# Recommendation model with target attention: the order of a pipelined kernel left to the tile scheduler, with the label's head and the top network no longer spread over steps

## The chip, the cores and the metric

The kernel runs on one core of a Trainium2 chip. The metric is device time in microseconds of one execution. A core has five engines that each work through their own queue of instructions in order and wait for each other on semaphores: TensorE (PE, matmuls; its weight loads are shown apart as PEld), VectorE (DVE), ScalarE (ACT), GpSimd (POOL, which here issues the indirect gathers) and SyncE (SP, which issues plain DMAs). TensorE reads SBUF and writes PSUM; VectorE and ScalarE read PSUM.

## The reference

For each of 16384 samples there are 69 item numbers and one label. Cut to what matters:

```python
u  = emb[batch_user]                      # (16384, 69, 96)
ql = emb[batch_label[:, 0]]               # (16384, 96)
z  = concat([q, u, q - u, q * u], -1)     # q is ql, repeated for the 69 items
h  = dice(z @ W1 + b1, a1)                # 64 wide
att = (h @ W2 + b2) @ W3 + b3             # one number for each item
pre = where(batch_user < ITEM_NUM, u * att, 0)
pooled = einsum('gf,bfe->bge', window, pre)   # ten groups of items, sums
x = concat([pooled, ql], -1)              # 11 * 96 wide
h = dice(bn(x @ Wf1 + bf1), af1)          # 200 wide
h = dice(bn(h @ Wf2 + bf2), af2)          # 80 wide
return h @ Wf3 + bf3
```

`dice(x, a)` is `x * (a + (1 - a) * sigmoid(x))` up to a tiny constant. All data is float32.

## The kernel before

The samples are taken in 128 blocks of 128; eight blocks make a round, whose item and label numbers are loaded with one DMA (`load_ids`, L416; `round_of`). A block has 69 tiles of 128 items. The tiles go in 18 chunks of four (the last two have three and two), and two chunks make a pair: nine pairs a block, 1152 in all. In names such as "pair 3" the pair's place in its block is meant, from 0 to 8.

Since `z @ W1` is linear in `u` for a fixed label, each sample has its own matrix: `A + Wp * q`, 96 x 64, with a row for the part that depends on the label alone. These matrices are `M`, one tile of 97 x 128 x 64 for a block, in two buffers. VectorE fills it in five pieces with two instructions each (`build`, L257 and L263), cut by the table `BUILD`. Ahead of that comes the label's head: the gather of the label's rows (`head_gather`), their transpose and its copy to `qT` (`head_turn`, L237 and L239), and the row `c` (`head_row`, L245 and L247), which goes through DRAM to the last row of `M` (L249 and L251, both issued by SP).

A pair goes through these steps:

- `fetch`: eight gathers by POOL into `u` (L222, ten buffers), each of 128 rows; eight transposes by TensorE into `ptr` (L274, PSUM, two buffers); two copies by ScalarE to one of four `uT` (L276).
- `hidden`: one product for each sample that the pair touches, with the sample's matrix as weights, into `ph` (L288); the two chunks use the two column halves of TensorE in turn. ScalarE makes `g` in two steps (L304, L305), VectorE makes `y` (L306).
- `attend`: TensorE makes `patt` (L316), VectorE makes `w` and `rw` (L326, L334).
- `pool`: TensorE multiplies `u` with `rw` into `acc` (L358), which gathers the group sums; VectorE copies a full `acc` to `pooled` (L366). With this the buffer of `u` is free for the gathers ten pairs on.

After a block's last pair the top network follows: `top1` (L377 on TensorE, L385 to L389), `top2` (L397 to L401), `top3` (L406, L408). All of `patt`, the head's products and those of the top network share two PSUM buffers of one tag, `m`.

The loop at the end of the kernel writes the order of the work by hand. It stands in `with tc.manual_schedule():`, in which each engine's queue has its instructions in the order of the program text. Step `i` does `pool` of pair i-3, `attend` of pair i-2, `hidden` of pair i-1, then, where a block ended, one of the top network's three parts (at distances 4, 5 and 6), then `fetch` of pair i. The next block's head goes at the end of the steps with pair 2, 3 and 4, its builds at the end of those with pairs 4 to 8. So in TensorE's queue each step has eight `acc`, four `patt`, some 17 `ph` and eight transposes (the first three in two passes each).

Of the kernel before, what the change touches and what calls it, by code (L numbers as in the profile page):

```python
# [30 lines left out]
F32 = mybir.dt.float32  # L31
# [24 lines left out]
NPR = NCH // 2  # L56
NCOL = NB * (NT + 1)

BUILD = {4: (0, 26), 5: (26, 52), 6: (52, 78), 7: (78, 103), 8: (103, 128)}

GROUPS = [(0, 43), (43, 86), (86, 128)]

# [23 lines left out]
def rec_kernel(  # L86
# [23 lines left out]
    nc = tc.nc  # L110
# [101 lines left out]
    bpool = ctx.enter_context(tc.tile_pool(name="bpool", bufs=2))  # L212
# [6 lines left out]
    ps_m = ctx.enter_context(tc.tile_pool(name="ps_m", bufs=2, space=PSUM))  # L219

    def gather(dst, index):
        nc.gpsimd.indirect_dma_start(  # L222
            out=dst,
            out_offset=None,
            in_=emb,
            in_offset=bass.IndirectOffsetOnAxis(ap=index, axis=0),
        )

    def head_gather(n, ids):

        q = bpool.tile([P, E], F32, tag="q", name=f"q{n}")
        gather(q, ids[:, NB * NT + n % NB : NB * NT + n % NB + 1])
        return q

    def head_turn(n, q):
        pq = ps_m.tile([E, BLK], F32, tag="m", name=f"pq{n}")
        nc.tensor.transpose(pq, q, ident)  # L237
        qT = qpool.tile([E, BLK], F32, tag="qT", name=f"qT{n}")
        nc.vector.tensor_copy(qT, pq)  # L239
        return qT  # L240

    def head_row(n, qT):

        pc = ps_m.tile([BLK, H1], F32, tag="m", name=f"pc{n}")
        nc.tensor.matmul(pc, qT, Cq, start=True, stop=True)  # L245
        c = bpool.tile([BLK, H1], F32, tag="c", name=f"c{n}")
        nc.vector.tensor_add(c, pc, b1b)  # L247
        cd = dpool.tile([BLK, H1], F32, tag="cd", name=f"cd{n}")
        nc.sync.dma_start(out=cd, in_=c)  # L249
        M = bpool.tile([E + 1, BLK, H1], F32, tag="M", name=f"M{n}")  # L250
        nc.sync.dma_start(out=M[E : E + 1], in_=cd.rearrange("(o n) h -> o n h", o=1))  # L251
        return M

    def build(qT, M, a, b):

        m = M[0:E, a:b, :]
        nc.vector.tensor_tensor(  # L257
            m,
            Wp.to_broadcast([E, b - a, H1]),
            qT[:, a:b].rearrange("e (m o) -> e m o", o=1).to_broadcast([E, b - a, H1]),  # L260
            ALU.mult,
        )
        nc.vector.tensor_tensor(m, m, A.to_broadcast([E, b - a, H1]), ALU.add)  # L263

    def fetch(i, bi, pr, ids):

        u = upool.tile([P, 8, E], F32, tag="u", name=f"u{i}")
        uT = uTs[i % len(uTs)]
        for j in range(2):
            ch = CHUNKS[2 * pr + j]  # L270
            ptr = ps_tr.tile([E, 512], F32, tag="tr", name=f"ptr{i}_{j}")
            for k, t in enumerate(ch):
                gather(u[:, 4 * j + k, :], ids[:, bi * NT + t : bi * NT + t + 1])
                nc.tensor.transpose(ptr[:, k * P : (k + 1) * P], u[:, 4 * j + k, :], ident)  # L274
            n = len(ch) * P
            nc.scalar.copy(uT[0:E, j * 512 : j * 512 + n], ptr[:, 0:n])  # L276
        return u
# [90 lines left out]
                            acc[gi][:, 0 : (b - a) * G].rearrange("e (s g) -> e s g", g=G),  # L368
                        )

    def top1(n, pooled, qT):
        x1 = bpool.tile([DH, 2, BLK], F32, tag="x1", name=f"x1_{n}")
        g1 = bpool.tile([DH, 2, BLK], F32, tag="g1", name=f"g1_{n}")
        p1 = ps_m.tile([DH, 2, BLK], F32, tag="m", name=f"p1_{n}")
# [15 lines left out]
        return x1  # L390

    def top2(n, x1):
        x2 = bpool.tile([D2, BLK], F32, tag="x2", name=f"x2_{n}")
        g2 = bpool.tile([D2, BLK], F32, tag="g2", name=f"g2_{n}")
        p2 = ps_m.tile([D2, BLK], F32, tag="m", name=f"p2_{n}")
# [6 lines left out]
        return x2  # L402

    def top3(n, x2, res):
        p3 = ps_m.tile([1, BLK], F32, tag="m", name=f"p3_{n}")
        nc.tensor.matmul(p3, wf3, x2, start=True, stop=True)  # L406
        bi = n % NB
        nc.vector.tensor_scalar(res[:, bi * BLK : (bi + 1) * BLK], p3, bf3c, None, ALU.add)  # L408
        if bi == NB - 1:
            nc.sync.dma_start(out=out_v[n // NB : n // NB + 1], in_=res)  # L410

    out_v = out.rearrange("(n b) o -> n (o b)", n=NIT)

# [2 lines left out]
        nc.sync.dma_start(out=ids, in_=idx[it : it + 1].rearrange("o p n -> (o p) n"))  # L416
        return ids

    rounds = {}

    def round_of(n):

        it = n // NB
        if it not in rounds:
            ids = load_ids(it)
            mask = ipool.tile([P, NB * NT], F32, tag="mask", name=f"mask{it}")
            nc.vector.tensor_scalar(mask, ids[:, 0 : NB * NT], float(ITEM_NUM), None, ALU.is_lt)
            rounds[it] = ids, mask, ipool.tile([1, NB * BLK], F32, tag="res", name=f"res{it}")
        return rounds[it]

    total = NBLK * NPR
    qs, qTs, Ms, us, ys, rws, accs, x1s, x2s = ({} for _ in range(9))

    def part(i, back):

        return divmod(i - back, NPR) if 0 <= i - back < total else None

    with tc.manual_schedule():
        qs[0] = head_gather(0, round_of(0)[0])
        qTs[0] = head_turn(0, qs.pop(0))  # L440
        Ms[0] = head_row(0, qTs[0])
        for a, b in BUILD.values():
            build(qTs[0], Ms[0], a, b)
        for i in range(total + 6):
            if at := part(i, 3):
                n, pr = at
                if pr == 0:
                    accs[n] = {"pooled": bpool.tile([E, G, BLK], F32, tag="pooled", name=f"pooled{n}")}
                pool(i - 3, pr, us.pop(i - 3), rws.pop(i - 3), accs[n])
            if at := part(i, 2):  # L450
                n, pr = at
                rws[i - 2] = attend(i - 2, n % NB, pr, round_of(n)[1], ys.pop(i - 2))
            if at := part(i, 1):
                n, pr = at
                ys[i - 1] = hidden(i - 1, pr, Ms[n])
            if (at := part(i, 4)) and at[1] == NPR - 1:
                n = at[0]
                x1s[n] = top1(n, accs.pop(n)["pooled"], qTs.pop(n))
            if (at := part(i, 5)) and at[1] == NPR - 1:
                x2s[at[0]] = top2(at[0], x1s.pop(at[0]))  # L460
            if (at := part(i, 6)) and at[1] == NPR - 1:
                top3(at[0], x2s.pop(at[0]), round_of(at[0])[2])
            if at := part(i, 0):
                n, pr = at
                us[i] = fetch(i, n % NB, pr, round_of(n)[0])
                if n + 1 < NBLK:
                    if pr == 1:
                        round_of(n + 1)
                    if pr == 2:
                        qs[n + 1] = head_gather(n + 1, round_of(n + 1)[0])  # L470
                    if pr == 3:
                        qTs[n + 1] = head_turn(n + 1, qs.pop(n + 1))
                    if pr == 4:
                        Ms[n + 1] = head_row(n + 1, qTs[n + 1])
                    if pr in BUILD:
                        build(qTs[n + 1], Ms[n + 1], *BUILD[pr])


# [39 lines left out]
```

## Time and profile before

Three runs took 14158.46, 14157.09 and 14178.55 us (median 14158.46).

| | before |
|---|---|
| profiled execution's own time | 14158.46 us |
| its span, first to last instruction | 14156.7 us |
| instructions | 187662 |
| mean granted TensorE clock | 0.575 |
| TensorE matmuls, busy | 10058.7 us, 71% |
| POOL busy | 9627.4 us, 68% |
| VectorE busy | 4441.9 us, 31% |
| ScalarE busy | 3142.9 us, 22% |
| gathers of `u` | 8832, mean 1073 ns |
| gathers of `q` | 128, mean 1145 ns |
| DMA, mean | 33 GB/s |

In a group of the profile there stand the line, engine and operation, what is written and read, and the count; then busy time in us and the mean of one in ns; then the idle time of that engine just before such instructions, with what ended most of it. "issue" is time in which an engine waited for nothing that the profile shows, and "remote" stands where the releaser was not found. In a list of waits there stand the waiting engine and line, the releaser, total us, times, and the longest. In a timeline there stand start and length in us, then the idle time before and its releaser. In a table of windows there stand, for each stretch of the span, its length and each engine's busy time with the number of instructions.

### The profile page before, as it was taken

To read this page: it belongs to the slowest core of one execution; us is meant where nothing else is said; L and a number is where in the kernel's file an instruction comes from. 1 tells how busy PE (TensorE), PEld (TensorE's weight loads), DVE (VectorE), ACT (ScalarE), POOL (GpSimd) and SP (SyncE) were. 2 spreads that over 40 slices of the span, in tenths; PEclk is the share of its full clock that TensorE was granted. 3 is DMA by queue.
4 is the path that set the end of the run, shared out by engine and by line. 5 is a ranking of instruction groups with operands and counts; after the bars stand their busy time and mean duration, and the time that the engine had idled before them with its cause. 6 is when DMAs were issued, how large, how long until landed. Compare 5 with 4: busy or idle time off the path is not lost.

```text
span 14156.7 us, 187662 instructions
## 1 busy us (share of the span) xinstructions
PE 10058.7 (71%) x80260; PEld 9342.3 (66%) x80260; DVE 4441.9 (31%) x6564; ACT 3142.9 (22%) x5506; POOL 9627.4 (68%) x8966
## 2 busy tenths in 40 slices
PE   5776677766777677767776677767677677777777
PEld 4676666666676666666676666666666666666666
DVE  2332333323333233323333333323332333323332
ACT  1222222222222222222222222222222222222222
POOL 6667666666676666766667666666666666676665
PEclk8555555555555555555555555555555555555555
DMA  1111111111111111111111111111111111111111
GB/s 37 33 33 33 33 33 33 34 33 33 33 33 34 33 34 33 33 34 33 33 33 34 33 33 33 33 33 33 33 33 33 33 33 33 33 34 33 33 32 25
DMA packets 311848, 467.53 MB, mean 33 GB/s; under 512 B 164156, under 2 KB 165340, under 8 KB 310892
## 3 DMA queue, kind: packets, MB, share of 16 engines
q0 software_dynamic: 286720, 440.98, 14.9%
q1 hardware_dynamic: 22634, 13.19, 0.4%
q8 instruction: 636, 10.42, 0.3%
q10 hardware_dynamic: 1666, 1.37, 0.0%
q14 instruction: 192, 1.57, 0.0%
HBM read 450.69 MB, written 4.26 MB: 32 GB/s over the span
## 4 chain that ended last, share of the span: by engine, by line
PE 41%; another core or an unknown queue 20%; POOL 17%; issue 12%; DVE 5%; ACT 3%; DMA 2%; SPq 0%; POOLq 0%; ACTq 0%; DVEq 0%
POOL u L222 17%; PE acc L358 10%; PE ph L288 9%; PE patt L316 8%; PE ptr L274 7%; PE p L377 4%; DMA u<-in_emb,ids 1%; DVE M L263 1%; DVE M L257 1%; DVE y L306 1%; ACT g L305 1%; ACT uT L276 1%; PE p L397 1%; ACT g L304 1%
## 5 line engine op out<-in xcount | busy, mean ns | idle before, releaser
L222 POOL DMA_INDIRECT u<-in_emb,ids x8832 | 9480.2, 1073 | 4261.9 <-issue 2428.5
L316 PE MATMUL patt<-v,y 128*128 128x2 f32 x8704 | 1814.7, 327 | 2543.8 <-DVE y L306 1985.8
L316 PEld LDWEIGHTS patt<-v,y 128*128 128x128 f32 x8704 | 1758.8, 297 | 2594.3 <-DVE y L306 2035.9
L288 PE MATMUL ph<-uT,M 97*64 97x69 f32 (+7 forms) x37120 | 2540.4, 304 | 897.9 <-issue 639.5
L358 PEld LDWEIGHTS acc<-rw,u 128*96 128x96 f32 x18176 | 2658.1, 241 | 571.2 <-issue 473.0
L288 PEld LDWEIGHTS ph<-uT,M 97*64 97x64 f32 x37120 | 2302.0, 213 | 1038.9 <-issue 736.5
L358 PE MATMUL acc<-rw,u 128*96 128x30 f32 (+2 forms) x18176 | 2689.7, 305 | 377.7 <-issue 344.1
L306 DVE TENSOR_TENSOR y<-ph,g 128x512 f32<-128x512 f32 (+2 forms) x1280 | 832.6, 650 | 6602.4 <-ACT g L305 3979.5
L304 ACT ACTIVATE g<-ph 128x512 f32<-128x512 f32 (+2 forms) x1280 | 722.1, 564 | 9052.7 <-remote 4204.1
L274 PE MATMUL ptr<-ident,u 128*96 128x128 f32 x8832 | 2075.7, 399 | 220.6 <-issue 162.2
L274 PEld LDWEIGHTS ptr<-ident,u 128*96 128x96 f32 x8832 | 1501.2, 184 | 473.5 <-issue 250.8
L276 ACT COPY uT<-ptr 96x512 f32<-96x512 f32 (+2 forms) x2304 | 1214.8, 558 | 997.5 <-remote 608.6
L263 DVE TENSOR_TENSOR M<-M,A 96x1664 f32<-96x1664 f32 (+1 forms) x640 | 1190.8, 1861 | 22.1
L257 DVE TENSOR_TENSOR M<-w,qT 96x1664 f32<-96x1664 f32 (+1 forms) x640 | 1184.0, 1850 | 0.0
L305 ACT ACTIVATE g<-g,a1c,na1c 128x512 f32<-128x512 f32 (+2 forms) x1280 | 999.2, 781 | 43.1
L377 PE MATMUL p<-pooled,wf 96*100 96x128 f32 x5120 | 930.9, 359 | 14.2 <-issue 12.7
L377 PEld LDWEIGHTS p<-pooled,wf 96*100 96x100 f32 x5120 | 881.9, 238 | 22.4 <-issue 17.9
L326 DVE SCALAR_TENSOR_TENSOR w<-patt,bb,mask 128x8 f32<-128x8 f32 (+2 forms) x1280 | 275.4, 215 | 1080.4 <-remote 515.1
L366 DVE COPY pooled<-acc 96x430 f32<-96x430 f32 (+1 forms) x384 | 337.8, 880 | 758.4 <-remote 718.1
L334 DVE TENSOR_TENSOR rw<-R,w 128x240 f32<-128x240 f32 (+2 forms) x1280 | 481.2, 376 | 43.8
L222 POOL DMA_INDIRECT q<-in_emb,ids x128 | 146.6, 1145 | 172.2 <-DMA ids<-in_idx 116.7
L385 DVE TENSOR_SCALAR x<-p,sbf 100x128 f32<-100x128 f32 x256 | 78.0, 346 | 589.0 <-PE ptr L274 534.1
(51 smaller groups left out, 1589.6 us busy)
## 6 DMA issues: line engine op xcount, KB each, us to landing
u<-in_emb,ids POOLq DMA_INDIRECT x8832
ids<-in_idx SPq DMA_DIRECT2D x16, 280.0 KB
cd<-c SPq DMA_DIRECT2D x128, 32.0 KB
M<-cd SPq DMA_DIRECT2D x128, 32.0 KB
q<-in_emb,ids POOLq DMA_INDIRECT x128
wf<-in_Wf ACTq DMA_DIRECT2D x1, 825.0 KB
wt<-in_wtok ACTq DMA_DIRECT2D x1, 345.0 KB
out<-res SPq DMA_DIRECT2D x16, 4.0 KB
```

Source lines behind the costliest of these rows:

```text
L222: nc.gpsimd.indirect_dma_start(out=dst, out_offset=None, in_=emb, in_offset=bass.IndirectOffsetOnAxis(ap=index, axis=0),)
L257: nc.vector.tensor_tensor(m, Wp.to_broadcast([E, b - a, H1]), qT[:, a:b].rearrange("e (m o) -> e m o", o=1).to_broadcast([E, b - a, H1]), ...
L263: nc.vector.tensor_tensor(m, m, A.to_broadcast([E, b - a, H1]), ALU.add)
L274: nc.tensor.transpose(ptr[:, k * P : (k + 1) * P], u[:, 4 * j + k, :], ident)
L276: nc.scalar.copy(uT[0:E, j * 512 : j * 512 + n], ptr[:, 0:n])
L288: nc.tensor.matmul(ph[j * H1 : (j + 1) * H1, a:b], M[:, s, :], uT[:, j * 512 + a : j * 512 + b], start=True, stop=True,)
L304: nc.scalar.activation(gs, ph[lo:hi, 0:n], AF.Sigmoid, scale=S_DICE)
L305: nc.scalar.activation(gs, gs, AF.Identity, bias=a1c[lo:hi], scale=na1c[lo:hi])
L306: nc.vector.tensor_mul(y[lo:hi, 0:n], ph[lo:hi, 0:n], gs)
L316: nc.tensor.matmul(patt[:, :, i], y[:, cols], v2, start=True, stop=True)
L358: nc.tensor.matmul(acc[gi][:, (x - a) * G : (z - a) * G], u[:, 4 * j + i, :], rw[:, j, i, (x - lo) * G : (z - lo) * G], start=False, stop= ...
L377: nc.tensor.matmul(p1[:, i, :], wf1[:, k, i * DH : (i + 1) * DH], pooled[:, k, :] if k < G else qT, start=(k == 0), stop=(k == G),)
```

## The change

The computation, its tiles and its buffers stay. `manual_schedule` goes: the tile framework's scheduler now orders each engine's instructions, from the priority of their place in the text and from what it expects to be ready. The text itself is in four stages: step `i` has the next block's head and build, then `hidden` of pair i-1, `attend` of pair i-2, `pool` of pair i-3, and `fetch` of pair i. The three head functions become one, `block_head`, at pair 2; the three parts of the top network become one, `top_net`, right after the block's last `pool`. `BUILD` has six pieces of 21 or 22 samples at pairs 3 to 8, in place of five of 25 or 26 at pairs 4 to 8.

```diff
-BUILD = {4: (0, 26), 5: (26, 52), 6: (52, 78), 7: (78, 103), 8: (103, 128)}
+BUILD = {3: (0, 22), 4: (22, 43), 5: (43, 64), 6: (64, 85), 7: (85, 106), 8: (106, 128)}
...
-    def head_gather(n, ids):
-
+    def block_head(n, ids):
+
+        bi = n % NB
         q = bpool.tile([P, E], F32, tag="q", name=f"q{n}")
-        gather(q, ids[:, NB * NT + n % NB : NB * NT + n % NB + 1])
-        return q
-
-    def head_turn(n, q):
+        gather(q, ids[:, NB * NT + bi : NB * NT + bi + 1])
         pq = ps_m.tile([E, BLK], F32, tag="m", name=f"pq{n}")
         nc.tensor.transpose(pq, q, ident)
         qT = qpool.tile([E, BLK], F32, tag="qT", name=f"qT{n}")
         nc.vector.tensor_copy(qT, pq)
-        return qT
-
-    def head_row(n, qT):
-
         pc = ps_m.tile([BLK, H1], F32, tag="m", name=f"pc{n}")
...
-        return M
+        return qT, M
...
-    def top1(n, pooled, qT):
...
+    def top_net(bi, pooled, qT, res):
...
-    total = NBLK * NPR
-    qs, qTs, Ms, us, ys, rws, accs, x1s, x2s = ({} for _ in range(9))
...
-    with tc.manual_schedule():
-        qs[0] = head_gather(0, round_of(0)[0])
-        qTs[0] = head_turn(0, qs.pop(0))
-        Ms[0] = head_row(0, qTs[0])
-        for a, b in BUILD.values():
-            build(qTs[0], Ms[0], a, b)
-        for i in range(total + 6):
-            if at := part(i, 3):
...
-                pool(i - 3, pr, us.pop(i - 3), rws.pop(i - 3), accs[n])
-            if at := part(i, 2):
...
-            if at := part(i, 1):
...
-            if (at := part(i, 4)) and at[1] == NPR - 1:
-                n = at[0]
-                x1s[n] = top1(n, accs.pop(n)["pooled"], qTs.pop(n))
-            if (at := part(i, 5)) and at[1] == NPR - 1:
-                x2s[at[0]] = top2(at[0], x1s.pop(at[0]))
-            if (at := part(i, 6)) and at[1] == NPR - 1:
-                top3(at[0], x2s.pop(at[0]), round_of(at[0])[2])
-            if at := part(i, 0):
-                n, pr = at
-                us[i] = fetch(i, n % NB, pr, round_of(n)[0])
-                if n + 1 < NBLK:
-                    if pr == 1:
-                        round_of(n + 1)
-                    if pr == 2:
-                        qs[n + 1] = head_gather(n + 1, round_of(n + 1)[0])
-                    if pr == 3:
-                        qTs[n + 1] = head_turn(n + 1, qs.pop(n + 1))
-                    if pr == 4:
-                        Ms[n + 1] = head_row(n + 1, qTs[n + 1])
-                    if pr in BUILD:
-                        build(qTs[n + 1], Ms[n + 1], *BUILD[pr])
+    blocks[0] = block_head(0, round_of(0)[0])
+    for a, b in BUILD.values():
+        build(*blocks[0], a, b)
+    total = NBLK * NPR
+    us, ys, rws, accs = {}, {}, {}, {}
+    for i in range(total + 3):
+        if i < total:
+            n, pr = divmod(i, NPR)
+            if pr == 1 and n + 1 < NBLK:
+                round_of(n + 1)
+            if pr == 2 and n + 1 < NBLK:
+                blocks[n + 1] = block_head(n + 1, round_of(n + 1)[0])
+            if pr in BUILD and n + 1 < NBLK:
+                build(*blocks[n + 1], *BUILD[pr])
+        if 0 <= i - 1 < total:
+            n, pr = divmod(i - 1, NPR)
+            ys[i - 1] = hidden(i - 1, pr, blocks[n][1])
+        if 0 <= i - 2 < total:
+            n, pr = divmod(i - 2, NPR)
+            rws[i - 2] = attend(i - 2, n % NB, pr, round_of(n)[1], ys.pop(i - 2))
+        if 0 <= i - 3 < total:
+            n, pr = divmod(i - 3, NPR)
...
+            pool(n, pr, us.pop(i - 3), rws.pop(i - 3), accs[n])
+            if pr == NPR - 1:
+                res = round_of(n)[2]
+                top_net(n % NB, accs.pop(n)["pooled"], blocks.pop(n)[0], res)
+                if n % NB == NB - 1:
+                    nc.sync.dma_start(out=out_v[n // NB : n // NB + 1], in_=res)
+        if i < total:
+            n, pr = divmod(i, NPR)
+            us[i] = fetch(i, n % NB, pr, round_of(n)[0])
```

More of the change, by code (lines that the diff above doesn't have):

```diff
@@ L369, in pool @@
                         )
-    def top1(n, pooled, qT):
-        x1 = bpool.tile([DH, 2, BLK], F32, tag="x1", name=f"x1_{n}")
-        g1 = bpool.tile([DH, 2, BLK], F32, tag="g1", name=f"g1_{n}")
-        p1 = ps_m.tile([DH, 2, BLK], F32, tag="m", name=f"p1_{n}")
+    def top_net(bi, pooled, qT, res):
+        x1 = bpool.tile([DH, 2, BLK], F32, tag="x1", name=f"x1_{bi}")
+        g1 = bpool.tile([DH, 2, BLK], F32, tag="g1", name=f"g1_{bi}")
+        p1 = ps_m.tile([DH, 2, BLK], F32, tag="m", name=f"p1_{bi}")
         for i in range(2):
@@ L389, in top1 @@
         nc.vector.tensor_mul(x1, x1, g1)
[L390 to L395, printed above, removed]
+        x2 = bpool.tile([D2, BLK], F32, tag="x2", name=f"x2_{bi}")
+        g2 = bpool.tile([D2, BLK], F32, tag="g2", name=f"g2_{bi}")
+        p2 = ps_m.tile([D2, BLK], F32, tag="m", name=f"p2_{bi}")
         for i in range(2):
@@ L401, in top2 @@
         nc.vector.tensor_mul(x2, x2, g2)
-        return x2
-    def top3(n, x2, res):
-        p3 = ps_m.tile([1, BLK], F32, tag="m", name=f"p3_{n}")
+        p3 = ps_m.tile([1, BLK], F32, tag="m", name=f"p3_{bi}")
         nc.tensor.matmul(p3, wf3, x2, start=True, stop=True)
-        bi = n % NB
         nc.vector.tensor_scalar(res[:, bi * BLK : (bi + 1) * BLK], p3, bf3c, None, ALU.add)
-        if bi == NB - 1:
-            nc.sync.dma_start(out=out_v[n // NB : n // NB + 1], in_=res)
     out_v = out.rearrange("(n b) o -> n (o b)", n=NIT)
@@ L417, in load_ids @@
         return ids
-    rounds = {}
+    rounds, blocks, steps = {}, {}, []
     def round_of(n):
@@ L429, in round_of @@
         return rounds[it]
+    blocks[0] = block_head(0, round_of(0)[0])
+    for a, b in BUILD.values():
+        build(*blocks[0], a, b)
     total = NBLK * NPR
-    qs, qTs, Ms, us, ys, rws, accs, x1s, x2s = ({} for _ in range(9))
-    def part(i, back):
-        return divmod(i - back, NPR) if 0 <= i - back < total else None
-    with tc.manual_schedule():
-        qs[0] = head_gather(0, round_of(0)[0])
-        qTs[0] = head_turn(0, qs.pop(0))
-        Ms[0] = head_row(0, qTs[0])
-        for a, b in BUILD.values():
-            build(qTs[0], Ms[0], a, b)
-        for i in range(total + 6):
-            if at := part(i, 3):
-                n, pr = at
-                if pr == 0:
-                    accs[n] = {"pooled": bpool.tile([E, G, BLK], F32, tag="pooled", name=f"pooled{n}")}
-                pool(i - 3, pr, us.pop(i - 3), rws.pop(i - 3), accs[n])
-            if at := part(i, 2):
-                n, pr = at
-                rws[i - 2] = attend(i - 2, n % NB, pr, round_of(n)[1], ys.pop(i - 2))
-            if at := part(i, 1):
-                n, pr = at
-                ys[i - 1] = hidden(i - 1, pr, Ms[n])
-            if (at := part(i, 4)) and at[1] == NPR - 1:
-                n = at[0]
-                x1s[n] = top1(n, accs.pop(n)["pooled"], qTs.pop(n))
-            if (at := part(i, 5)) and at[1] == NPR - 1:
-                x2s[at[0]] = top2(at[0], x1s.pop(at[0]))
-            if (at := part(i, 6)) and at[1] == NPR - 1:
-                top3(at[0], x2s.pop(at[0]), round_of(at[0])[2])
-            if at := part(i, 0):
-                n, pr = at
-                us[i] = fetch(i, n % NB, pr, round_of(n)[0])
-                if n + 1 < NBLK:
-                    if pr == 1:
-                        round_of(n + 1)
-                    if pr == 2:
-                        qs[n + 1] = head_gather(n + 1, round_of(n + 1)[0])
-                    if pr == 3:
-                        qTs[n + 1] = head_turn(n + 1, qs.pop(n + 1))
-                    if pr == 4:
-                        Ms[n + 1] = head_row(n + 1, qTs[n + 1])
-                    if pr in BUILD:
-                        build(qTs[n + 1], Ms[n + 1], *BUILD[pr])
@@ new lines, in rec_kernel @@
+    us, ys, rws, accs = {}, {}, {}, {}
[16 more added lines that the diff above has]
+            n, pr = divmod(i - 3, NPR)
+            if pr == 0:
+                accs[n] = {"pooled": bpool.tile([E, G, BLK], F32, tag="pooled", name=f"pooled{n}")}
+            pool(n, pr, us.pop(i - 3), rws.pop(i - 3), accs[n])
[7 more added lines that the diff above has]
+            us[i] = fetch(i, n % NB, pr, round_of(n)[0])
```

## The prediction, made before the changed kernel was run

> **What bounds the kernel now.** First the page, for the load of each engine and the gather group; then the one source line of the gathers; then the waits and the timeline around one block boundary; last a table of windows.
>
> ```profile
> PE 10058.7 (71%) x80260; PEld 9342.3 (66%) x80260; DVE 4441.9 (31%) x6564; ACT 3142.9 (22%) x5506; POOL 9627.4 (68%) x8966
> ...
> L222 POOL DMA_INDIRECT u<-in_emb,ids x8832 | 9480.2, 1073 | 4261.9 <-issue 2428.5
> ...
> L222 POOL DMA_INDIRECT q<-in_emb,ids x128 | 146.6, 1145 | 172.2 <-DMA ids<-in_idx 116.7
> ```
>
> ```profile
> L222 POOL DMA_INDIRECT u<-in_emb,ids x8832: 942/947/2758, 19.4 to 14061.2; - x197
> ```
>
> No engine is full, but POOL is nearly so: each gather has 0.30 us of issue before it (timeline), which the busy column leaves out. POOL's queue is then a complete account of the span: 18.0 us to the first gather; 8960 gathers at the undisturbed 0.947 + 0.30 = 1.247 us, 11173; slowing, 9480.2 + 146.6 - 8960 x 0.947 = 1142; waits, 4261.9 + 172.2 - 16.7 (start) - 8960 x 0.30 = 1729; 94.5 us after the last gather. The sum is 14157, against a span of 14156.7, a profiled time of 14158.46 and a median of 14158.46, so I sum on the span and add 2. Per block of 128 samples, of which there are 128: 87.3 pace + 8.9 slowing + 13.5 waits = 109.7 us. The waits are for slots of `u` (ten pairs), which the pooling matmuls free: POOL waits for TensorE. The tail has about one block of TensorE work (pooling of nine pairs) from 14068.9 to 14156.7, with no gathers: 88 us. So neither alone gives 110.
>
> ```profile
> ACT g L304 <- remote: 4204.1, 252, 50.1
> ```
>
> ```profile
> 6989.78 1.22 PE L288 MATMUL ph<-uT,M 97*64 97x69 f32 x32
> ...
> 7020.35 0.60 ACT L304 ACTIVATE g<-ph 128x512 f32<-128x512 f32 x1 [30.84 <-remote]
> ...
> 7031.97 0.95 POOL L222 DMA_INDIRECT u<-in_emb,ids  x1 [5.78 <-remote]
> ```
>
> ```profile
> core 0: us, PE busy (x) PEld busy (x) DVE busy (x) ACT busy (x) POOL busy (x), PEclk, DMA share, GB/s
> 6989.00:7020.00 31.00, 6.50 (x56) 4.79 (x56) 0.82 (x4) 0.51 (x2) 23.50 (x25) 0.53 0.19 40
> 7033.00:7057.00 24.00, 20.88 (x159) 19.30 (x156) 2.71 (x7) 5.08 (x9) 14.19 (x15) 0.64 0.16 34
> 7070.00:7112.00 42.00, 41.26 (x316) 39.05 (x315) 26.73 (x30) 13.21 (x23) 33.47 (x26) 0.50 0.15 32
> ```
>
> The reader is to see a coupling. In the first window POOL issues 25 gathers in 31 us (one in 1.25), TensorE gets 56 matmuls through, and a `ph` whose record ends by 6991 releases ScalarE only at 7020.35. In the third, VectorE builds the next block's `M`, gathers are slow (26 in 42 us), and TensorE is busy 41.3 of 42 us. So TensorE lags when gathers run at full pace, and runs free under builds or POOL pauses. The profile does not say why; I take it as a rule of this trace.
>
> [...] 0.95 us becomes 1.6 to 2.4 during L257/L263. [...]
>
> **A rule to cost by.** Let W be TensorE's work per block without gathers (88 us), b the time under builds, p POOL's pauses, f the share of its speed that TensorE keeps otherwise. Before: builds go with pairs 4 to 8, b = 42 (the window), p = 13.5: 42 + 13.5 + f x 54.2 = 88, f = 0.60, an average (the first window alone shows far less). With T = 96.2 + p the rule gives T = 109.7 + (W - 88) - 0.4 x (b - 42): a microsecond that TensorE loses costs one, one more under builds gives back 0.4 of one.
>
> **The change, part by part.** The formula, tiles, matmuls (45188 TensorE instructions as built in each), gathers, ScalarE work and pools stay. Removed: the hand order, so the scheduler orders each engine; the staging of the label's head over pairs 2, 3, 4 and of the top network over three later steps. Added: six builds of 21 or 22 samples for five of 25 or 26, two more VectorE instructions each block.
>
> 1. *Builds.* 1.88 us at 1664 elements and 1.82 at 1600 give 0.94 ns an element and 0.31 us fixed (estimate): twelve take 18.55 + 2 x 0.31 = 19.2 us. VectorE is 31% busy, so the 0.6 is hidden there; POOL's slowing grows by 0.6/18.55 of 8.9, 0.3 us. Without cover it costs 0.6 x 128 = 80 us.
>
> 2. *Where builds stand.* In the built order (block 60, steady) eight of twelve stand between `y` of pair 0 and `w` of pair 1, the rest singly as far as `y` of pair 6. The cluster goes with this TensorE work: 28 transposes at 0.24 = 6.8, the top network 9, two and a half `ph` at 2.2 = 5.5, one pooling 2.7, one `patt` 1.8: 26 us; four singles with 8 us each are 32. If a single covers half its pair, b = 26 + 16 = 42: no change. Bounds: 37 to 50, +2.0 to -3.2 us a block.
>
> 3. *Pooling later.* `acc` of pair 1 now comes after transposes of pair 6, where it trailed by three pairs. Between `acc` of pairs 0 and 1 stand about 23 us of TensorE work; POOL has one free pair there, 8 x 1.25 + slowing, up to 15 us. It pauses about 8 us, then three poolings come close together and it has none. Pauses are p; the rule has them, so nothing is added.
>
> 4. *Queue order on TensorE.* Before, `acc` and `patt` (4.5 us) stand between a pair's transposes and its `ph`, which hides the copy to `uT`. Now, for pairs 4, 7 and 8 and the next block's pair 1, two to four transposes do (0.5 to 1 us). The copy is 0.58 us and ScalarE may have 1.4 us of `g` ahead of it. Exposed: 0 to 1.5 us each, 3 us for four. `p2` and `p3` stand on TensorE, with the next `ph` behind them, and wait for VectorE's `x`, which stands behind builds of 1.5 us; `pc` waits for `qT`. By the rows they come 2 to 5 us early, so free; cover gone, two builds each, 3 us. I take 3 us together with the delay of releases at full pace. W grows by 6; bounds 0 (all covered) and 18 (each of six hand-offs meets a 3 us delay).
>
> 5. *Head and label lists.* The label gather moves one pair earlier in POOL's queue. SP issues the store of `c` and the load of `M`'s row (0.34 and 0.24 us, SP otherwise idle) a few pairs earlier, so the load of the label and token lists behind them in SP's queue is earlier. Gathers wait for it 116.7 us now; I take 60 off, bounds 0 and 117. PSUM tag `m` (two buffers) has the same users.
>
> Ends (18 + 94.5) I leave; a restart could move them by 20.
>
> Sum: 109.7 + 0.3 + 6 = 116.0 us; 6.3 x 128 = 806 - 60 = +746: 14157 + 746 + 2 = 14905, say 14900.
>
> **Rivals.** *A, forecast, 45%*: exposed hand-offs, 14900 (own range 14350 to 15500, W +2 to +11). For: TensorE has no slack under builds (41.3 of 42). Against: their size is an estimate.
>
> *B, the order does not matter, 20%*: gathers and matmuls share a fixed supply, and waits only move: 14150, range 14000 to 14300. For: POOL absorbs every wait today.
>
> *C, faster, 17%*: the cluster falls on pairs 1 to 3, which now run beside full-pace gathers, so b = 50 with the hand-offs covered: 109.7 + 0.3 - 3.2 = 106.8, -371 - 117: 13670. It decides once the exposed hand-offs are under 0.4 x 8 = 3.2 us a block, the lists left out.
>
> *D, much slower, 18%*: every hand-off meets a delayed release, W +18: 18.3 x 128 = 2342: 16500. For: ScalarE waits up to 50.1 us today. [...]
>
> **Chances and range.** Three runs span 21 us (0.15%), so 0.2% is about what can be told from no change. Faster: C and 6 of B, 23%; same: 5 of B; slower: A, D and 9 of B, 72%. From 13800 (half of C left out) to 16200 (most of D left out) is about 8 in 10.
>
> **What would show it.** Right: POOL's waits well over 1729 us; TensorE `ph` idle for `uT` over 247; slowing near 1180; still long "remote" waits of `g`. Wrong: POOL waits under 1729 (C), or the same total with other releasers (B). Wrong altogether: if TensorE's lag has nothing to do with the gathers' pace, or POOL finds slots free and the span nears 96.2 x 128.

## The result, and the profile after

The changed kernel takes 15422.27 us (median of four runs, 15411.57 to 15440.14) where the kernel before takes 14157.77 (median of four): ratio 1.0892, 95% interval 1.0873 to 1.0911. The profiled execution took 15432.39 us, its span is 15430.6 us, the mean granted TensorE clock 0.553 (0.575 before). One fact has to stand ahead of all else, because the numbers can't be understood without it: the chips that this study met are of two kinds. On three occasions (that of the result among them) the kernel before takes 14158 to 14185 us, on three others 12433 to 12445. I call them the first and the second kind. The prediction was made from a profile of the first kind. The chips of five occasions are known and are five different ones; which one gave the result is not on record, and no known chip was met twice. So whether a kind is a lasting property of a chip or a condition that it was in, these runs can't tell. A lower granted clock is not what makes the first kind slow: it is 0.569 to 0.579 in the runs of the kernel before there and 0.558 to 0.563 on the second kind.

First the load, from the page of the kernel after, the label's gather from its list of POOL's groups, and the gathers by their source line.

```profile
PE 10992.0 (71%) x80260; PEld 9675.6 (63%) x80260; DVE 4366.2 (28%) x6820; ACT 3144.4 (20%) x5506; POOL 9384.9 (61%) x8966
...
L222 POOL DMA_INDIRECT u<-in_emb,ids x8832 | 9262.4, 1049 | 5891.1 <-issue 2335.0
```

```profile
L222 POOL DMA_INDIRECT q<-in_emb,ids x128 | 121.9, 952 | 55.7 <-issue 38.7 <-DVE mask L414 17.0
```

```profile
L222 POOL DMA_INDIRECT u<-in_emb,ids x8832: 942/947/2398, 19.7 to 15331.4; - x197
...
  PE acc L352: 1711.6, 257
  PE ptr L268: 1268.1, 246
```

POOL's account, made as for the kernel before: slowing 9262.4 + 121.9 - 8960 x 0.947 = 899 us (1142 before); waits 5891.1 + 55.7 - 17.0 - 8960 x 0.30 = 3242 (1729); 98 us after the last gather (94.5); the pace is the same 11173. So of the 1274 us by which the span grew, 1513 are more waiting for slots of `u` and 243 less slowing. The wait for the list of items, 116.7 us before, is gone from the group of `q`.

The chain of work that ended last shows the same. Here are its shares by engine from the two pages, before and then after: TensorE has 59% of it (41% before), POOL 0% (17%).

```profile
PE 41%; another core or an unknown queue 20%; POOL 17%; issue 12%; DVE 5%; ACT 3%; DMA 2%; SPq 0%; POOLq 0%; ACTq 0%; DVEq 0%
```

```profile
PE 59%; another core or an unknown queue 21%; issue 15%; ACT 3%; DVE 1%; POOL 0%; DMA 0%; ACTq 0%; DVEq 0%
```

In the list of waits of the kernel after, the remote waits of `g` grew from 4204.1 us, and `w` of VectorE has as many again, where before it had 515.

```profile
DVE w L320 <- remote: 5610.4, 348, 29.9
ACT g L298 <- remote: 5181.3, 391, 34.2
...
PE ph L282 <- ACT uT L270: 595.7, 233, 26.0
```

The next fence has lines of the timeline of the kernel after, from a block in the middle of the run.

```profile
7462.30 1.55 DVE L257 TENSOR_TENSOR M<-M,A 96x1344 f32<-96x1344 f32 x1
7462.74 1.93 POOL L222 DMA_INDIRECT u<-in_emb,ids  x1 [0.30 <-issue]
...
7464.98 0.94 POOL L222 DMA_INDIRECT u<-in_emb,ids  x1 [0.30 <-issue]
...
7468.51 0.27 PE L282 MATMUL ph<-uT,M 97*64 97x69 f32 x1 [0.23 <-issue]
...
7469.90 0.50 PE L282 MATMUL ph<-uT,M 97*64 97x69 f32 x3 [1.12 <-issue]
...
7476.99 0.38 PE L310 MATMUL patt<-v,y 128*128 128x2 f32 x2 [1.94 <-issue]
7477.49 0.95 POOL L222 DMA_INDIRECT u<-in_emb,ids  x1 [0.31 <-issue]
7477.69 0.16 PE L310 MATMUL patt<-v,y 128*128 128x2 f32 x1 [0.32 <-issue]
7478.74 0.95 POOL L222 DMA_INDIRECT u<-in_emb,ids  x1 [0.30 <-issue]
...
7485.56 0.60 ACT L298 ACTIVATE g<-ph 128x512 f32<-128x512 f32 x1 [22.15 <-remote]
7485.66 0.23 DVE L320 SCALAR_TENSOR_TENSOR w<-patt,bb,mask 128x8 f32<-128x8 f32 x1 [21.81 <-remote]
7485.80 1.61 DVE L251 TENSOR_TENSOR M<-w,qT 96x1408 f32<-96x1408 f32 x1
7487.64 0.95 POOL L222 DMA_INDIRECT u<-in_emb,ids  x1 [5.45 <-PE ptr L268]
```

The reader is to see one stall whole. One build instruction at 7462.30 slows one gather (1.93 us), and the next gather is back at 0.94. While POOL then gathers at its full pace, TensorE comes forward by one to three matmuls at a time; `g` and `w` are released after 22 us, when POOL has no slot left and pauses (5.45 us). The next piece of `M`, which would have slowed a gather as the one at 7462.30 did, stands on VectorE behind that `w` and starts only at 7485.80. In the kernel before, all pieces stood together after the one long stall of a block; here two of the twelve build instructions wait a stall out. Two windows of the same block give the contrast, the cluster of builds and the stall:

```profile
7410.00:7434.00 24.00, 21.95 (x203) 19.74 (x203) 15.94 (x20) 7.42 (x14) 16.75 (x14) 0.71 0.15 33
7462.00:7485.00 23.00, 9.72 (x58) 7.98 (x58) 1.85 (x3) 0.58 (x1) 15.61 (x16) 0.50 0.17 36
```

TensorE (the first pair after the length) does 203 matmuls in 24 us of the one and 58 in 23 us of the other. Counted over the whole trace by the interval between the starts of two gathers (full pace under 1.27 us, slowed to 2.8, paused above), in us a block, with matmul records for each us in brackets:

| | full pace | slowed | paused |
|---|---|---|---|
| before, first kind of chip | 67.9 (4.99) | 23.4 (8.96) | 18.5 (4.03) |
| after, first kind | 67.9 (4.43) | 20.7 (8.29) | 31.1 (4.83) |

The block is longer by the pauses alone (12.6 us), and has 2.7 us less in which TensorE runs free. The mean granted clock in these stretches is 0.563, 0.557 and 0.637 before, and 0.524, 0.613 and 0.574 after.

### The profile page after: what moved, and what is told of

It is laid out like the page before. It is cut to its first block, busy times and chain, and to the rows that moved or that the text cites. A ratio compares the mean times of both kernels' runs of the same rounds, so it can differ in the third digit from the quotient of the medians.

```text
span 15430.6 us, 187044 instructions
## 1 busy us (share of the span) xinstructions
PE 10992.0 (71%) x80260; PEld 9675.6 (63%) x80260; DVE 4366.2 (28%) x6820; ACT 3144.4 (20%) x5506; POOL 9384.9 (61%) x8966
## 4 chain that ended last, share of the span: by engine, by line
PE 59%; another core or an unknown queue 21%; issue 15%; ACT 3%; DVE 1%; POOL 0%; DMA 0%; ACTq 0%; DVEq 0%
PE acc L352 16%; PE ph L282 15%; PE patt L310 10%; PE ptr L268 10%; PE p L371 6%; ACT uT L270 1%; ACT g L298 1%; PE acc L348 1%; PE p L389 1%; DVE pooled L360 1%; PE pc L239 1%; PE p L396 0%; ACT g L299 0%; POOL u L222 0%
## 5 line engine op out<-in xcount | busy, mean ns | idle before, releaser
L222 POOL DMA_INDIRECT u<-in_emb,ids x8832 | 9262.4, 1049 | 5891.1 <-issue 2335.0
L352 PE MATMUL acc<-rw,u 128*96 128x30 f32 (+2 forms) x18176 | 3050.3, 325 | 1923.3 <-issue 867.4
L352 PEld LDWEIGHTS acc<-rw,u 128*96 128x96 f32 x18176 | 2954.1, 263 | 2064.6 <-issue 898.6
L282 PE MATMUL ph<-uT,M 97*64 97x69 f32 (+7 forms) x37120 | 3037.2, 305 | 1534.4 <-issue 784.7
L282 PEld LDWEIGHTS ph<-uT,M 97*64 97x64 f32 x37120 | 2504.4, 209 | 2295.9 <-issue 1212.6
L268 PE MATMUL ptr<-ident,u 128*96 128x128 f32 x8832 | 2391.9, 393 | 219.5 <-issue 86.7
L310 PEld LDWEIGHTS patt<-v,y 128*128 128x128 f32 x8704 | 1978.3, 323 | 618.5 <-issue 575.5
L257 DVE TENSOR_TENSOR M<-M,A 96x1344 f32<-96x1344 f32 (+1 forms) x768 | 1204.5, 1569 | 0.0
L251 DVE TENSOR_TENSOR M<-w,qT 96x1344 f32<-96x1344 f32 (+1 forms) x768 | 1196.5, 1571 | 4.2
L348 PE MATMUL acc<-zrow 1*96 1x430 bf16 (+1 forms) x384 | 210.4, 548 | 136.5 <-issue 69.7
```

The source lines that it names most:

```text
L222: nc.gpsimd.indirect_dma_start(out=dst, out_offset=None, in_=emb, in_offset=bass.IndirectOffsetOnAxis(ap=index, axis=0),)
L251: nc.vector.tensor_tensor(m, Wp.to_broadcast([E, b - a, H1]), qT[:, a:b].rearrange("e (m o) -> e m o", o=1).to_broadcast([E, b - a, H1]), ...
L282: nc.tensor.matmul(ph[j * H1 : (j + 1) * H1, a:b], M[:, s, :], uT[:, j * 512 + a : j * 512 + b], start=True, stop=True,)
L310: nc.tensor.matmul(patt[:, :, i], y[:, cols], v2, start=True, stop=True)
L352: nc.tensor.matmul(acc[gi][:, (x - a) * G : (z - a) * G], u[:, 4 * j + i, :], rw[:, j, i, (x - lo) * G : (z - lo) * G], start=False, stop= ...
```

## The experiments

All orders below are written out by hand as one list of steps for a block. Each engine's queue was laid out as in the built kernel that it is named after, for the steady blocks. In such a list, `t:0.1` is the transposes of chunk 1 of pair 0, `h` is `ph`, `s` the pooling into `acc`, and a star gives the number of instructions:

```diff
-    for i in range(total + 3):
-        ...
+    for n in range(NBLK + 1):
+        for word in ORDER.split():      # "t:0.0*3 h:-1*10 G:-1 a:-2*4 ... h:7*16 G:7 a:6*4 ..."
+            token(n, word)
```

**TensorE's own time.** Both orders without the token gathers, to see what TensorE needs by itself.

```diff
-        T["u", i] = upool.tile([P, 8, E], F32, tag="u", name=f"u{i}")
+        T["u", i] = u_fixed
...
-                gather(T["u", i][:, 4 * j + k, :], round_of(n)[0][:, c : c + 1])
```

> Every engine's order is that of the kernel before, written out as one list of steps for a block; the 69 token gathers of each block are left out (all pairs read eight tiles gathered once, so the output is another one), the gather of the labels stays. What is left is TensorE's own time W. My theory (W = 88 us a block, read from the tail): 88 x 128 + 20 = about 11300 us. Rival, W is larger than that and the gathers cost nothing: over 13000 us. Long remote waits of g at line-by-line level (4204 us before) should be gone, under 500 us, in my theory.

> The same with the order of the changed kernel, engine by engine as it was built, and its six builds; token gathers left out in the same way. My theory, exposed hand-offs make W itself longer: 94 to 98 us a block, 12050 to 12560 us, 6 to 11% over the order of before without gathers. Rival, the hand-offs cost only beside gathers (releases come late there): within 2% of the order of before without gathers, about 11300 us.

9020.21 us for the order of before, 10024.98 for that of after: 70 and 78 us a block. The level of my W (88) was wrong by 18 us; what the order adds, 7.9 us a block, is near the 6 that I forecast. Beside these runs the kernel before took 12432.51 us, which was the first sight of the second kind of chip. There a block takes 97 us. In the order of before on such a chip (part 1 of the last run below) POOL waits for no slot: its pace, 87.3, and slowing, 9.2, nearly make up the block.

**A pause after each gather.** Two runs on a chip of the second kind, and two more on one of the first.

```diff
                 gather(T["u", i][:, 4 * j + k, :], round_of(n)[0][:, c : c + 1])
+                nc.gpsimd.memset(pause, 0.0)      # 128 x 32
```

> The order of before with all gathers, and on POOL's queue a small memset (128x32) after each token gather, 8832 of them, so that no two gathers follow each other at the full pace of 1.25 us. My theory, the pace of the gathers holds TensorE up: TensorE's releases come earlier (remote waits of g fall from 4204 us to under 2500), and though POOL has some 0.1 to 0.2 us more to do for each gather, the time stays at or below 14150 us (13300 to 14200). Rival, POOL's queue sets the time and the pace has no effect on TensorE: each memset adds its own 0.1 to 0.2 us, 15000 to 15900 us.

> The order of after with the same memset after each token gather. My theory: below 15420 us, 13800 to 15100, with POOL's waits for slots (3242 us) down by more than the memsets add. Rival, POOL's queue adds up whatever TensorE does: 16300 to 17200 us.

> The order of before with a memset (128x32, 0.14 us) on POOL's queue after each token gather, once more, since the chips differ: it took 12513 us where before took 12433. On a chip where before takes about 14170 us: if the uninterrupted pace of the gathers is what holds TensorE's releases up, the memsets break it and the time is 12500 to 13200 us; rival, the stalls are a property of that chip's gathers whatever stands between them: 13900 to 14500 us.

> The order of after with the same memsets; it took 12598 us where before took 12433. On a chip where before takes about 14170 us: 12600 to 13400 us if the memsets break the stalls, 15100 to 15700 us in the rival. Where before takes 12433 again: 12598.

Second kind: 12513.31 and 12597.75 us, 1.0064 (1.0047 to 1.0081) and 1.0133 (1.0116 to 1.0150) of before. First kind: 14252.60 and 15205.75, 1.0052 (1.0036 to 1.0068) and 1.0728 (1.0703 to 1.0754). The experiment did not do what it was made for: the memset went into the time that had been issue. POOL's timeline of the order of before with pauses, on the second kind:

```profile
7000.02 0.95 POOL L216 DMA_INDIRECT u<-in_emb,ids  x1 [0.16 <-issue]
7000.97 0.15 POOL L245 MEMSET pause<- 128x32 f32 x1
7001.28 0.95 POOL L216 DMA_INDIRECT u<-in_emb,ids  x1 [0.17 <-issue]
```

The pace stayed at 1.26 us, so nothing follows on a slower pace. But the pair of runs shows something better: one program, the same pace of gathers, and on one chip no stall. From the waits of this kernel, first on the second kind and then on the first:

```profile
ACT g L285 <- PE ph L266: 5664.9, 1144, 7.0
```

```profile
ACT g L285 <- remote: 4083.8, 251, 50.2
ACT g L285 <- PE ph L266: 1224.2, 339, 33.5
POOL u L216 <- remote: 800.4, 272, 5.5
POOL u L216 <- PE acc L353: 673.7, 161, 12.5
```

No release of `g` later than 7.0 us on the one, up to 50.2 on the other. Full-pace gathers are not enough for a stall; something that differs between the two kinds has to be there too.

**Both kernels again, as they are.**

> The changed kernel once more, without an edit, beside the kernel before on the same chip: the last four runs had the kernel before at 12433 us, not 14158, so the chips differ. If the loss of the change is TensorE's own work (78 us a block against 70 without gathers, 8 x 128 = 1000 us) and the order of before is now set by POOL's queue (12433 us is 97 us a block), then after is POOL's pace too, or little more: 12400 to 13000 us where before takes 12433. If the loss is in stalls beside the gathers on every chip: 9% over before again, 13500 where before takes 12433, 15420 where it takes 14158.

> The kernel before, for its profile on this chip. If the chip is one where it takes 12433 us: POOL's waits for slots near zero (1729 us in the first profile), no release of g later than 10 us (50.1 us), remote waits of g under 500 us (4204). If it is one where it takes 14158 us, the first profile again.

> The changed kernel without an edit, beside the two. Where before takes about 14170 us: 15420, a third time. Where before takes 12433: if after loses only through stalls that this chip doesn't have, POOL's pace sets it, 12450 to 12700 us; if TensorE's longer own time shows too, 12900 to 13500 us.

On two more occasions of the first kind, on two different chips: after 15418.36 and 15356.05 us, ratios 1.0884 (1.0857 to 1.0912) and 1.0833 (1.0805 to 1.0860). The kernel before at 14174.42 has the stalls of its first profile (remote waits of `g` 4308.7 us). The loss goes with the kind; it is not that of a single chip.

**TensorE's queue put together again.** After's order with each pair's transposes and `ph` as one run; of the list, TensorE's steps alone, around pair 2 and 3.

```diff
-t:2.0*4 p1-1*22 t:2.1*4 h:2 s:0*8 t:3.0*2 h:2*16 t:3.0*2 t:3.1*4 p2-1*2 h:3 t:4.0*4 h:3*16 t:4.1*4
+t:2.0*4 t:2.1*4 c+1 h:1*17 a:0*4 p1-1*22 s:0*8 t:3.0*4 t:3.1*4 h:2*17 p2-1*2 t:4.0*4 t:4.1*4 h:3*17
```

> The order of after, but TensorE's queue put together again: the transposes of a pair as one run (9 runs a block, as before, where after has 26) and its ph as one run (9 for 21), each pair's transposes one place ahead of another group, so that the copy to uT is hidden. VectorE's order, the late pooling, the top network, the head and the six builds stay as in after. If the short runs and the exposed copies are what the change costs (7.8 us of TensorE work a block without gathers), the loss goes: where before takes about 14170 us, 14150 to 14550; where it takes 12433, 12400 to 12550. Rival, the late pooling and the places of the builds cost: 15000 to 15500 us, or 12600 and more on the other kind of chip.

12431.75 us, 0.9988 (0.9979 to 0.9996) of before, on a chip of the second kind, where it tells little: POOL's queue, 97 us a block, hides TensorE's own time (75 us for this order, 78 for that of after, in the last run below). This order has not run on the first kind, so what it would give back there is not known.

**Gathers slowed in earnest.**

```diff
-    pause = const.tile([P, 32], F32, name="pause")
+    pause = const.tile([P, 256], F32, name="pause")
```

> The order of before, with a larger memset (128x256, some 0.3 us by the 0.2 us of the 128x128 at the start) after each token gather: the 128x32 one fitted into the 0.30 us of issue and left the pace at 1.25 us; this one should make it about 1.41. Pace alone costs 70 x 1.41 + 8.9 = 107.6 us a block, 13800 us. If the pace of the gathers is what stalls TensorE where before takes 14170 us, the stalls go and it is 13750 to 14000, faster than before, with remote waits of g under 1500 us. Rival, the stalls stay at any pace: 15300 to 15900 us. Where before takes 12433: 13800 in both.

The chip was again of the second kind: 13967.02 us, near the 13800 of POOL's own sum. The two groups of POOL say why it is 170 more. With 953 ns (the median gather), 328 and 167 (1473.5 of issue over 8832) the pace is 1.45 us, not 1.41, which is some 335 us more; slowing, 9378.8 - 8832 x 0.953 = 962 us, is less than the 8.9 us a block (1139) of the sum, and gives half of that back.

```profile
L216 POOL DMA_INDIRECT u<-in_emb,ids x8832 | 9378.8, 1062 | 1497.7 <-issue 1473.5 <-PE ptr L251 24.2
L245 POOL MEMSET pause<- 128x256 f32 x8832 | 2900.0, 328 | 6.9
```

What a slower pace does on the first kind was not seen.

**Eight parts in one program.** The last run put all open questions side by side.

```diff
+# order, token gathers, elements of the memset after each
+PARTS = [
+    ('before', True, 0), ('after', True, 0), ('whole', True, 0), ('before', True, 256),
+    ('before', True, 512), ('before', False, 0), ('after', False, 0), ('whole', False, 0),
+]
```

> One program of eight parts of 16 blocks each, drained between them, read from its trace as microseconds a block (from one block's first copy to uT to the next one's, over the inner blocks of a part): 1 order of before, 2 order of after, 3 order of after with whole runs, 4 order of before with a 128x256 memset after each gather, 5 the same with 128x512, 6 to 8 the three orders without token gathers (there the output is another one). On a chip where before takes about 14170 us: part 1 110, part 2 120; part 3 110 to 113 if the short runs and exposed copies are the cost, 117 and more if the late pooling or the places of the builds are; part 4 108 to 110 and part 5 118 to 121 if the stalls go with the pace (POOL's own sum: 70 gathers at 1.41 or 1.56 us and 9), 118 to 123 and 128 to 135 if they stay. On a chip where it takes 12433: part 1 97, part 2 97 to 99, part 3 97, part 4 109, part 5 120. Parts 6 to 8 on either: 70, 78, and 70 to 72 for whole runs (77 and more in the rival).

Again a chip of the second kind (before 12441.59 us; the eight parts 11981.51). A part's time is read from the copies to `uT` that open its fourth and its last block, twelve blocks apart. For parts 1 and 2, from ScalarE's timeline:

```profile
332.74 0.58 ACT L298 COPY uT<-ptr 96x512 f32<-96x512 f32 x1
...
1494.76 0.58 ACT L298 COPY uT<-ptr 96x512 f32<-96x512 f32 x1
...
1883.87 0.58 ACT L298 COPY uT<-ptr 96x512 f32<-96x512 f32 x1 [1.60 <-PE ptr L293]
...
3051.94 0.58 ACT L298 COPY uT<-ptr 96x512 f32<-96x512 f32 x1 [1.60 <-PE ptr L293]
```

| part | us a block | expected on this kind |
|---|---|---|
| 1 order of before | 96.8 | 97 |
| 2 order of after | 97.3 | 97 to 99 |
| 3 whole runs | 96.4 | 97 |
| 4 before, gathers slowed | 108.6 | 109 |
| 5 before, slowed more | 121.5 | 120 |
| 6 before, no gathers | 70.0 | 70 |
| 7 after, no gathers | 77.9 | 78 |
| 8 whole runs, no gathers | 75.1 | 70 to 72 |

On the second kind the order of after costs 0.5 us a block, because POOL's 97 us cover TensorE's 78: POOL waits for no slot in either part, and its gathers are slowed by 9.7 us a block in part 2 and 9.2 in part 1. Part 8 missed: whole runs give back 2.8 of the 7.9 us, not all, and its blocks take 72.2 and 78.0 us in turn. The windows of parts 6, 7 and 8 (length, then TensorE's matmuls and weight loads):

```profile
8590.65:9430.28 839.63, 839.63 (x7526) 808.04 (x7526) 417.66 (x613) 291.81 (x517) 14.22 (x12) 0.62 0.02 4
9748.59:10682.80 934.21, 922.04 (x7526) 821.82 (x7526) 408.85 (x638) 291.74 (x516) 12.18 (x12) 0.61 0.01 3
10983.44:11884.53 901.09, 867.46 (x7526) 813.79 (x7525) 405.77 (x637) 298.97 (x516) 10.61 (x10) 0.61 0.01 3
```

The same 7526 matmuls take 840, 934 and 901 us, and leave TensorE idle for 0, 12 and 34 us of it: in part 7 little of the 95 us shows as idle time. From start to start of successive matmuls in the trace, a block has 46 changes from one kind of product to another in part 6, 75 in part 7, 42 in part 8, and these steps take 9.4, 18.9 and 12.5 us. The 14 a block that go from a transpose to `ph` in part 7 take 0.33 us each, while transposes of one run follow at 0.17.

These times mix two clocks. The granted clock of these parts is at every moment either 1.0 or 0.5, and a step takes about half as long at 1.0: poolings of one run follow at a median of 85 ns there and 160 at 0.5, transposes at 109 and 213. How much of each kind of work falls at 1.0 is not the same in the three parts (39%, 15% and 24% of the poolings), so I weight each moment with its granted clock, which gives microseconds of full clock (an estimate from the clock records and the starts of the matmuls: it counts waits for other engines as if they followed this clock, too):

| us of full clock a block | part 6 | part 7 | part 8 |
|---|---|---|---|
| all | 43.5 | 47.5 | 46.1 |
| changes of kind | 6.0 | 11.4 | 8.0 |
| transposes, inside runs | 6.6 | 5.0 | 6.6 |
| poolings, inside runs | 10.4 | 10.5 | 10.9 |
| mean granted clock | 0.622 | 0.610 | 0.614 |

Part 7 has 3.9 more than part 6. The changes have 5.4 more, of which 1.6 are transposes that stood inside runs before; the difference, 3.8, is nearly the whole. Poolings cost the same. At the clock of part 7 the 3.9 are 6.5 us; the other 1.4 of the 7.9 come from that clock being lower than part 6's (43.5 / 0.610 less 43.5 / 0.622). Of the 6.5, waits of the weight loads of `ph` for the copy to `uT` are 2.0 us (23.9 in twelve blocks), by the list of waits of part 7:

```profile
PEld ph L308 <- ACT uT L298: 23.9, 72, 0.6
```

Part 8 has fewer changes than part 6, and they still cost 2.0 us of full clock more. So it is not their number alone: three gaps a block over 0.6 us (into `p2`, into a new `acc`, into a pooling) take 3.7 us there, and stand at the late pooling and at the top network in one go. Nor do the two column halves that `ph` uses single out a change: in part 7 a step from a transpose to `ph` takes 0.33 us, but one from a transpose to a pooling, without column halves, takes 0.33 too, and one from `ph` to a transpose 0.17, as inside a run of transposes. What a change costs besides a wait for an operand, no run here shows.

## Why the prediction was right, and where its sizes were off

The direction and the forecast case, A, held: the order costs TensorE time (shown on the second kind of chip, without gathers), and on the first kind POOL's waits for slots grow. That the first is the cause of the second there is argued from the sum below, not shown by a run. 14900 us was 522 short of 15422. Step by step:

- *POOL's account and W.* The account of POOL's queue held. W = 88 us a block did not: the tail is a drain at whose end steps wait for each other (TensorE is idle for 9.3 of the 87.8 us, 2.6 of them before `p2` and 1.6 before `p3`), and TensorE's own time is 70 us. The forecast took only the growth of W, so the level did no harm to its sum; but f = 0.60 hung on it.
- *The rule.* That TensorE lags at full pace holds on three occasions and not on three others (`g` waits for up to 50.1 us in the first profile, for up to 7.0 in the order of before with pauses on the second kind). It was given as a rule of the trace, and that is all it is.
- *Step 1, builds.* The pieces take what was worked out (18.8 us a block for 19.2), but slowing came to 899 us, not 1180: pieces that run while POOL waits for a slot slow nothing, and 4.3 us of them a block do so, where before 1.0 did.
- *Step 2, where builds stand.* "b = 42: no change" failed. The time with slowed gathers fell from 23.4 to 20.7 us a block. At full pace TensorE had 4.99 / 8.96 = 0.56 of its rate, so 2.7 us less at the full rate is worth 0.44 x 2.7 = 1.2 us. In the block shown the cluster is about as long as thought (23 us for 26), but the single at 7462.30 covers little beyond its own 1.6 us.
- *Step 3, pooling later.* The pause at the first gather of pair 2, 8 us, measured 9.6 (4.3 before). That POOL then has none is not right: the first gathers of pairs 5 and 7 pause 4.6 and 2.9 us in the mean, where before neither paused 0.4. "Nothing is added" is not right either: with the runs whole and the pooling still late, part 8 keeps 5.1 us of the 7.9, and two of its three gaps stand at the pooling.
- *Step 4, queue order on TensorE.* The size was near, the make-up wrong: 6 us forecast, 7.9 measured on the second kind of chip and without gathers, of which 6.5 at an equal clock. Waits for the copy to `uT` come to 2.0 us a block, against 3 forecast for the copies. The other 3, waits of `p2`, `p3` and `pc`, don't show there: the steps into them take 0.7 us a block in part 7 and 0.8 in part 6. The larger part lies at the other changes of kind, which the prediction put at nothing: after has 26 runs of transposes and 21 of `ph` a block for 9 and 9. That the short runs are a cause is shown by part 8, which puts them together and is 2.8 us shorter. That 6 came so near is in part luck: half of it did not come, and a cost that was not foreseen stood in its place.
- *Step 5, head and lists.* Forecast -60 us, measured -117: the upper bound.

In sum 7.9 x 128 + 1.2 x 128 - 117 = 1048 us, of 1274 by which the span grew. This takes the 7.9 as if it held beside gathers on the first kind, which was not measured. Some 226 us, 1.8 us a block, stay open. Two things may have a part in them, and no run on the first kind took them apart. The mean granted clock is lower (0.553 against 0.575); whether that is a cause or comes from the stalls is not known. And the stalls have changed their form: the records show 651 stretches of over 6 us without a release of TensorE, 6611 us in all, where before had 318 with 4761. These are counted from incomplete records: of the releases due, 10285 of 11564 are in the trace of after and 12142 of 13178 in that of before.

Of the rivals, B (the order does not matter, since something else is fixed) is what happens on the second kind of chip, where POOL's queue is the fixed thing (order of after 1.0133 and of before 1.0064 of the kernel before, both with pauses). So that the forecast held hung also on the kind of chip that gave the result. C fell: the cluster on pairs 1 to 3 came, but it did not cover more, and the hand-offs were not under 3.2 us. D's price was not reached. Of the signs named ahead, POOL's waits, the idle time of `ph` for `uT` (595.7 us, 247.4 before) and the remote waits came; slowing did not.

What stays open is the cause of the stalls. It is shown that they need more than full-pace gathers, that they come on three occasions of six with the same program, and that the kernel before takes 1740 us more where they come (14180 against 12440). Whether a slower pace would end them was not tried there, and no order with all its gathers beat the kernel before by more than 0.2%.

## What to carry to other kernels

In these runs the order was paid for at the changes between kinds of product on TensorE: look at the runs in its queue, not only at its waits (46 changes a block against 75: 70 us against 78). Their number is a first sign and no price: an order with 42 took 75 us, with 3.7 us a block in three gaps at changes. Whether the order costs anything depends on what else bounds the block, and that can differ between chips: a 97 us queue on POOL hid 8 us of TensorE on the second kind, while on the first the same change cost 9.9 us a block. So take W from a run without the other engine's work, not from the tail of a trace, weight times on TensorE with the granted clock before two means are compared (here a pooling took 85 ns at 1.0 and 160 at 0.5), and ask for a second chip before a mechanism is called one of the hardware.

## What the runs showed that was not expected

- One program, two kinds of chips: 12433 to 12445 us on three occasions, 14158 to 14185 on three. The gathers have the same pace (1.25 us) on both, and the medians from start to start inside a run of transposes (213 ns) and of poolings (160 ns) beside gathers are the same; what differs is the late releases of TensorE.
- In the stall of the kernel after TensorE is not still: it comes forward by one to three matmuls every 0.7 to 2 us, with the gap put down to issue. The gaps have a grain. Of 2060 gaps of 0.6 to 1.6 us between starts of matmuls, 837 lie from 0.68 to 0.74 us and 549 from 1.38 to 1.44. One program, the order of after with pauses, has 632 and 393 of 1837 on the first kind, and 97 and 29 of 1332 on the second. What sets this grain is open.
- In the stall of the kernel before that the prediction shows, it is the releases that are late, more than the starts: matmuls with ten releases start from 6990.78 to 6999.46, and after 6990.73 the next release on record is at 7020.33; eleven come until 7031.80.
- On the first kind a part of TensorE's releases has no record: for the order of after with pauses, 10457 of 11521 are in the trace there, and all on the second kind. A wait put down to "remote" may be one whose release has no record.
- A 128x32 memset of 143 ns between two gathers costs next to nothing: it takes the place of as much of the 0.30 us of issue (pace 1.258 us against 1.252). A 128x256 one of 328 ns makes the pace 1.45.
- Poolings of one run follow each other at a mean of 126 ns in the order of before and 148 in that of after, without gathers and with a mean granted clock of 0.62 and 0.61. The cause is where they fall: 39% and 15% of them at a granted clock of 1.0 (median 85 ns), the others at 0.5 (160 ns). Two equal mean clocks do not make the means of one kind of work comparable.
